# A two-layer block of attention, FP4 feed-forward and a recurrence: rounding's small steps in another form, zeros written by ScalarE, and another order of hand-written plans

## The chip, the cores and the metric

The kernel runs on one core of one Trainium2 chip. The core has five engines that run their own queues in order and wait for each other by semaphores: TensorE (PE, with its weight loads as PEld), VectorE (DVE), ScalarE (ACT), GpSimd (POOL) and SyncE (SP), which here only issues DMAs. The metric is the device time of one execution in microseconds; lower is better.

## What is computed

Sixteen sequences of 512 tokens with 256 channels, all in fp32, pass four steps, each with a residual and a LayerNorm behind it:

```
x = LN(x + attention(x))       16 heads, through 32 latents per head, rotary, causal softmax
x = LN(x + fp4_ffn(x))         256 -> 704 (gate, up) -> 256
x = LN(x + recurrence(x))      512 steps, one after the other, 16 heads x 64 states
x = LN(x + channel_mix(x))     three 256x256 products, token shift
```

The feed-forward rounds its inputs, its hidden values and its weights to FP4 in blocks of 16 values:

```python
scale = max(abs(block)) / 6, at least 1e-12
q = nearest of {0, .5, 1, 1.5, 2, 3, 4, 6} to abs(block / scale), with its sign, times scale
```

The recurrence is `state = tanh(state @ tanh(a) + x_t @ b)`; its result is `state @ c + skip * x_t`.

## The kernel before

**Two stages.** In the first, attention and feed-forward run over the sequences b = 0 to 15. In the second, the recurrence steps through time for all sequences at once and the channel mix runs beside it. Between them lies the rest of the last sequence's feed-forward. The result of the first stage goes through DRAM (`xs`) from one to the other.

**Slots.** A sequence's attention is 12 slots: four groups g of heads, each with three blocks n of query rows. A slot computes four heads' scores (`scores`, L524, into four PSUM banks), DVE adds the mask and finds the row's extreme (L536), ACT takes the exponentials (L549), TensorE turns the probabilities (`turn`, L559) one slot later, ACT copies them (L561), and behind a group's third block `weighted` multiplies with the values (L590). All products of this stage share seven PSUM banks, drawn by `mm`.

**Plans.** Between these steps, twice per head, `Beside.half_slot` puts in other work from a list written by hand: `PLAN_0` and `PLAN_1` for the first two sequences, `PLAN_15` for the last, `PLAN` for the thirteen between (b = 2 to 14). An entry is a kind of task, the sequence it belongs to as an offset, and a part: "U-1.2" is the next step of the feed-forward's first half (`ffn_up`) for tokens 256 to 383 of the sequence before this one. The kinds: L latents, H heads, V values, O output projection with LayerNorm (L497 to L504), Q quantization of the feed-forward's input, U gate and up products, D down product with LayerNorm (L331, L98) and the store to `xs` (L334), P a pause. A "U" has three entries: it transposes (ps_xq), then makes the first half's gate and up products (pg, pu), then the second half's. A "D" has two: transposes of the hidden values (ps_h, copied to hT), then the product (ps_d). An entry that has more than one step is called again at its next place in the list.

**What sets the order.** TensorE runs its instructions in the order in which the program is written (`manual_schedule`). The instructions of the other engines are ordered by a scheduler that takes what is ready by its own account, earlier lines first; so they may run well ahead of the place in the program at which they stand. `Q` only queues the rounding; its pieces are written out one per half slot by `vector_step`, and the rest at once by `vector_done` when a U or D step needs them.

**Rounding.** `fp4` (L181) is a chain on one engine after another: DVE takes the block maxima (L201), scales them and bounds them from below (L202), inverts (L203), multiplies by a constant just under 1 (L204), multiplies the data by the inverse (L207), makes a rounding constant (L209, L210) and adds it (L213); POOL subtracts it (L214) and multiplies by the scale (L215).

**LayerNorm.** DVE's statistics (L91, L92), POOL's reciprocal root (`rstd_of`, L84 and L86), and one DVE instruction for (x - mean) * rstd: L98 in `layernorm`, L502 in `out_projection`.

**Between the stages.** The list `FIRST` holds the steps for the last sequence that run before the recurrence: E quantize now, U and D as above, F wait for a hidden rounding, N the recurrence's first normalized tokens (`normed`). Then the recurrence's first input products (L1020) begin. `hist`, four tiles that hold states, is zeroed at L1008.

Of the kernel before, what the change touches and what calls it, by code (L numbers as in the profile page):

```python
# [10 lines left out]
F32 = mybir.dt.float32  # L11
# [3 lines left out]
AF = mybir.ActivationFunctionType  # L15
ALU = mybir.AluOpType
# [43 lines left out]
def tile_kernel(ctx: ExitStack, tc: tile.TileContext, I: dict, out: bass.AP):  # L60
# [8 lines left out]
    neg_half = const.tile([P, 4], F32, name="neg_half")  # L69
    nc.gpsimd.memset(neg_half, -0.5)  # L70
    cols = const.tile([P, NCOLS], F32, name="cols")
    nc.sync.dma_start(cols, I["cols"])
# [21 lines left out]
    def layernorm(dst, src):  # L94
        mv = small.tile([P, 4, 2], F32, tag="mv", name="mv")
        stats_into(mv[:, 0, :], src)
        rs = rstd_of(mv, 1, LN_EPS)
        nc.vector.tensor_scalar(dst, src, mv[:, 0, 0:1], rs[:, 0:1], ALU.subtract, ALU.mult)  # L98

# [81 lines left out]
    def fp4(dst, x, nb, rows=P):  # L181
# [13 lines left out]
        def blocks(t):  # L195
            return t.rearrange("p (n k) -> p n k", k=16)
# [4 lines left out]
        nc.vector.tensor_reduce(sc, blocks(x), AX.X, ALU.max, apply_absolute_value=True)  # L201
        nc.vector.tensor_scalar(sc, sc, 1.0 / 6.0, 1e-12, ALU.mult, ALU.max)  # L202
        nc.vector.reciprocal(inv, sc)  # L203
        nc.vector.tensor_scalar(inv, inv, 1.0 - 2.0**-23, None, ALU.mult)  # L204
        if n > C:
            yield
        nc.vector.tensor_tensor(blocks(q), blocks(x), over(inv), ALU.mult)  # L207
        yield
# [132 lines left out]
    with ExitStack() as a:  # L341
# [56 lines left out]
        vpad = [wts.tile([P, NT, H, 32], F32, name=f"vpad{i}") for i in range(2)]  # L398
        for i in range(2):
            nc.gpsimd.memset(vpad[i], 0.0)  # L400

# [80 lines left out]
        def out_projection(b):  # L482
# [3 lines left out]
            for j in range(0, NT, 2):  # L486
# [14 lines left out]
                for i in range(2):  # L501
                    nc.vector.tensor_scalar(  # L502
                        x[:, j + i, :], x[:, j + i, :], mv[:, i, 0:1], rs[:, i : i + 1],
                        ALU.subtract, ALU.mult,  # L504
                    )
# [110 lines left out]
        def pause(b):  # L616
# [15 lines left out]
        PLAN = [  # L632
            "L0.1", "L0.1", "U-2.3", "U-2.3", "H0", "H0", "O-1", "D-2.2", "L0.1", "O-1", "V1",
            "D-2.2", "L0.2", "L0.2", "L0.3", "Q-1.0", "L0.3", "Q-1.1", "L0.2", "U-1.0", "D-2.3",
            "U-1.1", "U-1.0", "U-1.0", "V1", "L0.3", "U-1.1", "Q-1.2", "H1", "U-1.2", "D-2.3",
            "Q-1.3", "U-1.2", "U-1.1", "U-1.2", "H1", "U-1.3", "D-1.0", "D-1.0", "D-1.1", "L1.0",
            "L1.0", "D-1.1", "L1.0",
# [14 lines left out]
        PLAN_15 = [  # L652
            "L0.1", "U-2.3", "U-2.3", "H0", "H0", "L0.1", "O-1", "D-2.2", "L0.1", "P0", "D-2.3",
            "L0.2", "D-2.2", "L0.3", "L0.2", "O-1", "Q-1.0", "U-1.0", "L0.2", "L0.3", "U-1.0", "P0",
            "P0", "Q-1.1", "U-1.0", "L0.3", "U-1.1", "U-1.1", "D-2.3", "Q-1.2", "Q-1.3", "P0",
            "U-1.2", "D-1.0", "U-1.3", "U-1.2", "P0", "U-1.1", "U-1.2", "D-1.0", "U-1.3", "U-1.3",
            "D-1.1", "D-1.1", "D-1.3", "D-1.2", "D-1.3", "D-1.2",
        ]
# [124 lines left out]
        ps_y = five.enter_context(tc.tile_pool(name="ps_y", bufs=1, space=PSUM))  # L783
        banks[:] = [ps_2] * 2 + [ps_b] * 5

        with tc.manual_schedule(engines={mybir.EngineType.PE}):
# [219 lines left out]
    for g in range(2):  # L1006
        for i in range(2):
            nc.gpsimd.memset(hist[g][i], 0.0)  # L1008
    state = [None, None]
# [65 lines left out]
    def beside(M):  # L1075
# [16 lines left out]
    FIRST = [  # L1092
        "E3", "U0", "U0", "E1", "U0", "U3", "U1", "U1", "D0", "E2", "F0", "D0", "U1", "U2", "N0",
        "U2", "U3", "F1", "U2", "N0", "F2", "U3",
    ]
# [203 lines left out]
```

## Time and profile before

| | |
|---|---|
| median of three runs | 2560.16 us (2558.01 to 2562.15) |
| the profiled execution | 2558.65 us, of it the span 2556.6 us |
| busy: PE, DVE, ACT, POOL | 2428.8, 1944.7, 1613.2, 1036.7 us |
| a middle sequence (892.9 to 1000.9) | 108.0 us, PE busy 105.99, DVE 89.00 |
| the last sequence (1650.6 to 1774.0) | 123.4 us, PE busy 112.63 |
| between the stages (1774 to 1828) | 54.0 us, PE busy 32.74 |
| the recurrence (1828 to 2556) | 728 us, PE busy 704.75, DVE 483.94 |

How to read it: times are microseconds from the span's start unless marked ns. A line of the order of time gives start, duration, engine, line, operation, out<-in, shapes and count; in brackets stand the engine's idle time before it and what ended that. A line of the groups gives, behind the count, busy microseconds and mean ns of one, then idle time before it and its releasers. A DVE or POOL instruction that waits for the other one's access to memory counts as busy while it waits. Matmuls are pipelined, and their ends are modelled. fp32 matmuls show as two instructions each.

### The profile page before, as it was taken

What the parts mean: (1) busy time and instruction counts of PE and PEld (TensorE: products, weight loads), DVE (VectorE), ACT (ScalarE), POOL (GpSimd) and SP (SyncE); (2) the same over time, 40 slices, a digit from 0 to 9 for tenths busy, and PEclk for the clock granted to TensorE, in tenths of its full rate; (3) what the DMA queues carried; (4) which work ended last, traced back from release to release, by engine and by line L of the source; (5) the groups of instructions that cost most, each with busy time, mean ns of one, the idle gap of its engine ahead of it and who ended that gap; (6) DMA issues with size and microseconds to landing.
All of it is one profiled execution on the core that took longest, in us unless ns stands there. A gap on an engine that the chain in (4) does not pass through costs nothing.

```text
span 2556.6 us, 73922 instructions
## 1 busy us (share of the span) xinstructions
PE 2428.8 (95%) x28802; PEld 1713.3 (67%) x28802; DVE 1944.7 (76%) x5621; ACT 1613.2 (63%) x5532; POOL 1036.7 (41%) x1649
## 2 busy tenths in 40 slices
PE   8789999999999999999999999997799999999998
PEld 4456666666666666666666666665578888888885
DVE  6767888788888888888787887877756666666666
ACT  4656666666666666667666666664266666666664
POOL 4322333333333333333333333333545555555554
PEclk9889999999999999999999999999899999999999
DMA  3000000000000000000000000000101111111100
GB/s 118 22 10 6 14 22 14 16 15 12 24 14 16 16 12 24 14 16 14 14 16 22 14 14 7 16 11 11 42 28 40 40 40 40 38 38 40 36 28 27
DMA packets 58016, 61.30 MB, mean 24 GB/s; under 512 B 7873, under 2 KB 53058, under 8 KB 57666
## 3 DMA queue, kind: packets, MB, share of 16 engines
q1 hardware_dynamic: 56802, 55.54, 7.1%
q8 instruction: 226, 3.70, 0.6%
q14 instruction: 124, 1.02, 0.1%
q10 hardware_dynamic: 864, 1.05, 0.1%
HBM read 39.79 MB, written 16.78 MB: 22 GB/s over the span
## 4 chain that ended last, share of the span: by engine, by line
PE 54%; DVE 28%; ACT 9%; POOL 5%; issue 3%; DMA 1%; ACTq 0%; DVEq 0%; POOLq 0%
PE u L1060 8%; DVE p L536 6%; PE ps_pt L559 5%; PE u L1020 5%; PE S L524 4%; ACT p L549 4%; PE py L590 3%; PE pg L160 3%; PE pu L160 3%; PE ps_h L439 3%; ACT pT L561 3%; DVE q_q L207 2%; PE ps_a L904 2%; PE ps_d L160 2%; DVE q_sc L201 2%
## 5 line engine op out<-in xcount | busy, mean ns | idle before, releaser
L549 ACT ACTIVATE p<-p,nm 128x512 f32<-128x512 f32 (+3 forms) x1024 | 569.9, 561 | 520.1 <-DVE nm L536 516.1
L1068 ACT ACTIVATE hist<-u 64x64 f32<-64x64 f32 x2048 | 445.5, 218 | 235.1 <-PE u L1060 153.0
L536 DVE CUSTOM_DVE_ANT_0 p<-S,mask 128x512 f32<-128x512 f32 (+3 forms) x1024 | 443.7, 483 | 50.2 <-PE S L524 50.2
L559 PEld LDWEIGHTS ps_pt<-ident,p 128*128 128x128 f32 x2560 | 296.5, 141 | 235.4 <-issue 85.5
L1060 PEld LDWEIGHTS u<-hist,ta 128*64 128x64 f32 x8176 | 367.3, 138 | 119.9 <-ACT hist L1068 40.7
L559 PE MATMUL ps_pt<-ident,p 128*128 128x128 f32 x2560 | 393.3, 280 | 9.0 <-DVE nm L536 3.5
L1060 PE MATMUL u<-hist,ta 128*64 128x32 f32 x8176 | 394.2, 218 | 4.6 <-ACT hist L1068 4.4
L561 ACT COPY pT<-ps_pt 128x384 f32<-128x384 f32 (+1 forms) x768 | 370.0, 515 | 39.2 <-PE ps_pt L559 38.9
L214 POOL TENSOR_TENSOR q_q<-q_q,q_m 128x256 f32<-128x256 f32 (+1 forms) x142 | 167.3, 1178 | 452.0 <-DVE q_q L213 434.4
L524 PE MATMUL S<-kc,qr 32*128 32x128 f32 (+3 forms) x2048 | 235.3, 474 | 8.9 <-ACT qr L478 7.9
L1020 PE MATMUL u<-xt,wb 128*64 128x64 f32 x4128 | 223.0, 230 | 2.4 <-issue 2.4
L549 ACT ACTIVATION_READ_ACCUMULATOR p<-p,nm 128x1 f32 x1024 | 199.3, 195 | 0.0
L160 PE MATMUL pg<-wgT,xqT 128*128 128x352 f32 x512 | 177.6, 470 | 4.1 <-ACT xqT L289 2.9
L473 POOL TENSOR_TENSOR qc<-qc,qs 128x512 f32<-128x512 f32 x64 | 81.5, 1274 | 236.3 <-DVE qs L472 231.3
L160 PE MATMUL pu<-wuT,xqT 128*128 128x352 f32 x512 | 172.8, 460 | 1.2 <-DVE th L304 1.2
L160 PE MATMUL ps_d<-wdT,hT 128*128 128x256 f32 x732 | 169.7, 381 | 2.2 <-ACT hT L323 2.2
L590 PEld LDWEIGHTS py<-pT,vpad 128*32 128x32 f32 x5120 | 141.2, 110 | 43.0 <-issue 30.7
L1020 PEld LDWEIGHTS u<-xt,wb 128*64 128x64 f32 x4128 | 164.9, 138 | 7.4 <-issue 3.0
L590 PE MATMUL py<-pT,vpad 128*32 128x128 f32 x5120 | 165.3, 276 | 3.8 <-ACT pT L561 3.5
L524 PEld LDWEIGHTS S<-kc,qr 32*128 32x128 f32 x2048 | 110.8, 185 | 78.0 <-issue 32.0
L84 POOL TENSOR_SCALAR ve<-mv 128x1 f32<-128x1 f32 (+1 forms) x160 | 32.6, 204 | 302.1 <-DVE mv L92 276.7
L160 PEld LDWEIGHTS ps_d<-wdT,hT 128*128 128x128 f32 x732 | 134.9, 191 | 19.6 <-ACT hT L323 3.1
(164 smaller groups left out, 4595.6 us busy)
## 6 DMA issues: line engine op xcount, KB each, us to landing
xT<-in_xT_dram SPq DMA_DIRECT2D x16, 512.0 KB
x<-in_x_dram SPq DMA_DIRECT2D x16, 512.0 KB
xs<-x SPq DMA_DIRECT2D x64, 128.0 KB
x<-xs SPq DMA_DIRECT2D x32, 256.0 KB
xm<-xs SPq DMA_DIRECT2D x32, 256.0 KB
out_dram<-o SPq DMA_DIRECT2D x64, 128.0 KB
w<-in_w_down_dram SPq DMA_DIRECT2D x2, 352.0 KB
w<-in_w_gate_dram SPq DMA_DIRECT2D x5, 128.0 KB
```

Of the source, the lines that this page charges most:

```text
L160: nc.tensor.matmul(dst, left, right, start=start, stop=stop)
L214: nc.gpsimd.tensor_tensor(q, q, m, ALU.subtract)
L473: nc.gpsimd.tensor_tensor(of[k], of[k], x, ALU.add)
L524: nc.tensor.matmul(S[h][:, at : at + w], q[rs, i * P : i * P + P], k[rs, :w], start=True, stop=True,)
L536: nc.vector.tensor_tensor_reduce(out=p[:, own], in0=S[h][:, own], in1=mask[:, T - (i + 1) * P :], scale=1.0, scalar=-MASKED, op0=ALU.add, ...
L549: nc.scalar.activation(p[:, own], p[:, own], AF.Exp, bias=nm[:, u : u + 1], scale=-1.0, accum_out=sum_of[b, g][:, cb, half, h : h + 1],)
L559: nc.tensor.transpose(ps[:, at : at + P], p[:, at : at + P], ident)
L561: nc.scalar.copy(pT[:, :w], ps[:, :w])
L590: nc.tensor.matmul(py[q * 32 : q * 32 + 32, PLACE[i][1], :], vpad[b % 2][:, j, g * 4 + h, :], pt, start=j == 0 and h % 2 == 0, stop=j == i ...
L1020: nc.tensor.matmul(u[rs, k, par:n:2, bs : bs + 16], wb[:, g * 2 + k, par, half, rs], xt[:, g, at : at + n - par : 2, :], start=par == 0 an ...
L1060: nc.tensor.matmul(into[cs, :, c, :], ta[:, t % 2, g * 2 + k, cs], own[:, :, c, :], start=False, stop=True, skip_group_check=True,)
L1068: nc.scalar.activation(state[g][rs, :, r * 32 : r * 32 + 32].rearrange("p k (s b) -> p k s b", s=2), u[rs, :, t - t0, :] .rearrange("p k ( ...
```

## The change

1. In `fp4`, L202 becomes a scalar_tensor_tensor with a constant tile `tiny` (1e-12) as its second tensor; L204 goes, and its constant moves into L207, which becomes a scalar_tensor_tensor. `tiny` is filled by one POOL memset at the start.
2. In `layernorm` and `out_projection`, L98 and L502 become scalar_tensor_tensor, with rstd spread over the row by a stride of zero as the second tensor.
3. The zeros of `vpad` (L400, POOL) are written further down in the program, just ahead of the loop over slots.
4. The zeros of `hist` (L1008) are written by ACT, as an Identity with scale 0 of the tile `ta`, instead of by POOL memsets.
5. `PLAN`, `PLAN_15` and `FIRST` get other orders. `PLAN` and `FIRST` hold the same entries as before; `PLAN_15` has one pause fewer.

```diff
+    tiny = const.tile([P, 44], F32, name="tiny")
+    nc.gpsimd.memset(tiny, 1e-12)
...
-        nc.vector.tensor_scalar(dst, src, mv[:, 0, 0:1], rs[:, 0:1], ALU.subtract, ALU.mult)
+        nc.vector.scalar_tensor_tensor(
+            dst, src, mv[:, 0, 0:1], rs[:, 0:1].to_broadcast([P, C]), ALU.subtract, ALU.mult
+        )
...
-        nc.vector.tensor_scalar(sc, sc, 1.0 / 6.0, 1e-12, ALU.mult, ALU.max)
+        nc.vector.scalar_tensor_tensor(sc, sc, 1.0 / 6.0, tiny[:rows, :nb], ALU.mult, ALU.max)
         nc.vector.reciprocal(inv, sc)
-        nc.vector.tensor_scalar(inv, inv, 1.0 - 2.0**-23, None, ALU.mult)
         if n > C:
             yield
-        nc.vector.tensor_tensor(blocks(q), blocks(x), over(inv), ALU.mult)
+        nc.vector.scalar_tensor_tensor(
+            blocks(q), blocks(x), 1.0 - 2.0**-23, over(inv), ALU.mult, ALU.mult
+        )
...
         vpad = [wts.tile([P, NT, H, 32], F32, name=f"vpad{i}") for i in range(2)]
-        for i in range(2):
-            nc.gpsimd.memset(vpad[i], 0.0)
...
-                    nc.vector.tensor_scalar(
-                        x[:, j + i, :], x[:, j + i, :], mv[:, i, 0:1], rs[:, i : i + 1],
-                        ALU.subtract, ALU.mult,
+                    nc.vector.scalar_tensor_tensor(
+                        x[:, j + i, :], x[:, j + i, :], mv[:, i, 0:1],
+                        rs[:, i : i + 1].to_broadcast([P, C]), ALU.subtract, ALU.mult,
                     )
...
         PLAN = [
-            "L0.1", "L0.1", "U-2.3", "U-2.3", "H0", "H0", "O-1", "D-2.2", "L0.1", "O-1", "V1",
-            "D-2.2", "L0.2", "L0.2", "L0.3", "Q-1.0", "L0.3", "Q-1.1", "L0.2", "U-1.0", "D-2.3",
-            "U-1.1", "U-1.0", "U-1.0", "V1", "L0.3", "U-1.1", "Q-1.2", "H1", "U-1.2", "D-2.3",
-            "Q-1.3", "U-1.2", "U-1.1", "U-1.2", "H1", "U-1.3", "D-1.0", "D-1.0", "D-1.1", "L1.0",
+            "L0.1", "L0.1", "U-2.3", "U-2.3", "H0", "H0", "O-1", "D-2.2", "L0.1", "D-2.2", "O-1",
+            "V1", "L0.2", "L0.2", "L0.3", "L0.3", "Q-1.1", "Q-1.0", "U-1.0", "L0.2", "U-1.1",
+            "D-2.3", "U-1.0", "U-1.0", "V1", "L0.3", "U-1.1", "H1", "Q-1.2", "U-1.2", "Q-1.3",
+            "D-2.3", "U-1.2", "U-1.1", "D-1.0", "U-1.2", "H1", "L1.0", "D-1.0", "D-1.1", "U-1.3",
             "L1.0", "D-1.1", "L1.0",
         ]
...
         PLAN_15 = [
-            "L0.1", "U-2.3", "U-2.3", "H0", "H0", "L0.1", "O-1", "D-2.2", "L0.1", "P0", "D-2.3",
-            "L0.2", "D-2.2", "L0.3", "L0.2", "O-1", "Q-1.0", "U-1.0", "L0.2", "L0.3", "U-1.0", "P0",
-            "P0", "Q-1.1", "U-1.0", "L0.3", "U-1.1", "U-1.1", "D-2.3", "Q-1.2", "Q-1.3", "P0",
-            "U-1.2", "D-1.0", "U-1.3", "U-1.2", "P0", "U-1.1", "U-1.2", "D-1.0", "U-1.3", "U-1.3",
-            "D-1.1", "D-1.1", "D-1.3", "D-1.2", "D-1.3", "D-1.2",
+            "L0.1", "L0.1", "U-2.3", "D-2.2", "U-2.3", "H0", "H0", "L0.1", "O-1", "D-2.2", "D-2.3",
+            "O-1", "L0.2", "Q-1.0", "U-1.0", "L0.3", "U-1.0", "Q-1.2", "Q-1.1", "L0.2", "L0.3",
+            "L0.2", "U-1.1", "P0", "P0", "U-1.0", "U-1.1", "U-1.2", "D-2.3", "U-1.2", "Q-1.3",
+            "L0.3", "U-1.3", "D-1.0", "U-1.1", "U-1.2", "D-1.0", "D-1.1", "U-1.3", "U-1.3", "D-1.1",
+            "P0", "D-1.2", "D-1.3", "D-1.2", "P0", "D-1.3",
         ]
...
         banks[:] = [ps_2] * 2 + [ps_b] * 5
+        for i in range(2):
+            nc.gpsimd.memset(vpad[i], 0.0)
...
     for g in range(2):
         for i in range(2):
-            nc.gpsimd.memset(hist[g][i], 0.0)
+
+            nc.scalar.activation(
+                hist[g][i].rearrange("p t k n -> p (t k n)"), ta.rearrange("p a k n -> p (a k n)"),
+                AF.Identity, scale=0.0,
+            )
...
     FIRST = [
-        "E3", "U0", "U0", "E1", "U0", "U3", "U1", "U1", "D0", "E2", "F0", "D0", "U1", "U2", "N0",
-        "U2", "U3", "F1", "U2", "N0", "F2", "U3",
+        "U0", "U0", "E1", "E3", "U0", "U3", "D0", "U1", "F0", "E2", "D0", "U1", "N0", "U2", "U1",
+        "F1", "U2", "U2", "U3", "U3", "F2", "N0",
     ]
```

## The prediction

> **What bounds the kernel now.** I read the page first (busy shares, then the chain that ended last), then busy time by stage, then who waits for whom in single stages, then the order of time where a stage's waits end.
>
> ```profile
> PE 2428.8 (95%) x28802; PEld 1713.3 (67%) x28802; DVE 1944.7 (76%) x5621; ACT 1613.2 (63%) x5532; POOL 1036.7 (41%) x1649
> ```
>
> TensorE is busy 95% of the span and nobody else over 76%. By stage (stretch, length, then busy time of PE, PE's weight loads, DVE, ACT and POOL, the granted clock, DMA):
>
> ```profile
> 892.90:1000.90 108.00, 105.99 (x850) 70.78 (x850) 89.00 (x266) 71.13 (x213) 37.40 (x45) 1.00 0.05 16
> 1650.60:1774.00 123.40, 112.63 (x961) 77.15 (x962) 93.44 (x283) 72.91 (x216) 38.98 (x49) 0.99 0.04 13
> 1774.00:1828.00 54.00, 32.74 (x110) 20.80 (x109) 40.45 (x98) 6.32 (x15) 22.81 (x30) 0.84 0.09 27
> ```
>
> A middle sequence (the first) takes 108 us and leaves TensorE 2.0 us idle; DVE has 19 us to spare. So TensorE bounds the thirteen sequences that PLAN orders, and VectorE's saving there is hidden unless TensorE waits for it. The last sequence leaves 10.8 us idle, the border between the stages (the rest of the last sequence's feed-forward) 21.3 of 54. From 1828 on is the recurrence, 728 us, which the change leaves alone. The gain can lie in three places only: 26 us of idle (plus part-idle, below) in the middle, 11 in the last sequence, 21 at the border.
>
> **The border.** In order of time:
>
> ```profile
> 1779.27 3.61 POOL L1008 MEMSET hist<- 128x1024 f32 x4
> 1779.36 3.98 DVE L502 TENSOR_SCALAR x<-x,mv,rstd 128x256 f32<-128x256 f32 x2 [0.43 <-POOL rstd L86]
> ...
> 1788.40 0.69 PE L287 MATMUL ps_xq<-ident,xq 128*128 128x128 f32 x2 [10.20 <-POOL xq L215]
> ```
>
> Two normalizations that take 0.41 us each elsewhere take 3.98 together: they sit until the four memsets end at 1782.88. TensorE waits 10.2 us for what follows. The chain that ended last runs through "POOL hist L1008 x4", 3.56 us. Moving the zeros to ACT removes the memsets: 3.98 becomes 2 x 0.475 = 0.95, so 3.0 us; one L204 less on this chain, 0.17. Gain 3.1. ACT pays 4 x 1.06 us (the 128x1024 ACTIVATE of ta took 1056 ns) but idles 14.7 us before its xqT copy at 1789; that covers the 4.2 us three times over. Without that cover it would cost up to 4.2, and the xqT copy would be late.
>
> FIRST's new order: U0's three steps, then D0 at once, before U1's products. In the trace D0's transposes waited 6.12 us for hq; ahead of them stood U1's products (2.63 us). Now only U3's transposes (0.4) stand there. hq comes after U0's last L307: 0.89+0.2+0.42+0.9+0.52+0.52+0.88 of DVE, 1.69+1.39 of POOL, some gaps: 7.8 us. It no longer shares DVE with U1's steps and x2's quantization (it took 9.6 us after the product's end, now 8.3). TensorE therefore waits about 8.0 instead of 6.1+0.5, but U1's 2.6 us are work that comes later and covers D0's normalization and its two transfers (L98's end at 1814.1 to the first L859 at 1819.1: 5.0 us). N0's transposes go last, so the L872 that fills xt (1.0 us) lies open before L1020. E3 goes behind E1: x3's rounding then fills DVE while U0's products run. Net -0.4, between -2.5 and +2. Moved with D0 is its store to xs on SP and the load after it; nothing else is queued on SP between them. **Border: -3.5 us.**
>
> **Rounding and normalizing on DVE.**
>
> ```profile
> L202 DVE TENSOR_SCALAR q_sc<-q_sc 128x44 f32<-128x44 f32 x66 | 27.7, 419 | 1.1
> L204 DVE TENSOR_SCALAR q_inv<-q_inv 128x16 f32<-128x16 f32 x74 | 31.2, 423 | 1.0
> L204 DVE TENSOR_SCALAR q_inv<-q_inv 128x44 f32<-128x44 f32 x66 | 24.0, 364 | 1.1
> L98 DVE TENSOR_SCALAR x<-x,mv,rstd 128x256 f32<-128x256 f32 x64 | 26.4, 413 | 74.1 <-POOL rstd L86 74.0
> L942 DVE SCALAR_TENSOR_TENSOR muk<-d,cols,x3T 128x256 f32<-128x256 f32 x64 | 28.0, 476 | 0.2
> ```
>
> L204's mean is 423 and 364 ns, its median 176: most of the mean is a wait for POOL inside the instruction. Two readings of that differ. If the new three-operand form never waits for POOL, the change saves L204 whole (55 us), L202's excess over 0.18 us (74 x 0.07 + 66 x 0.24 = 21 us) and L502's (mean 615, median 414: 64 x 0.2 = 13 us): 5.5 us per sequence. The Trainium skill, SBUF — State Buffer, section "Who interferes with whom", speaks against this: a DVE instruction with two SBUF inputs still contends with a GpSimd instruction that reads SBUF; only one that merely writes leaves it free. The trace agrees on an instruction with two SBUF inputs:
>
> ```profile
> 1804.41 1.38 POOL L215 TENSOR_TENSOR hq<-q_q,q_sc 128x704 f32<-128x704 f32 x1
> ...
> 1804.51 1.56 DVE L213 TENSOR_TENSOR q_q<-q_q,q_m 128x256 f32<-128x256 f32 x1
> ```
>
> This L213 takes 0.42 us when alone and 1.56 here, to just after POOL's end. All four new forms (L98, L202, L207, L502) read two SBUF tensors, and POOL's L214, L215 and L473 read SBUF. So I take it that the waits stay, or go on to L207 and L209, and that only L204's bare 0.16 to 0.18 us goes: 8 x 0.17 = 1.4 us per sequence.
>
> Against it stand the slower forms. By VectorE: DVE Perf Modes, section "The perf-mode tier table", fp32 tensor_scalar runs at twice the rate that a two-tensor operation has: 256/0.96/2 = 133 ns lost on each L98 and L502, 17 us in all. By the rows it is 476 - 413 = 63 ns, 8 us in all or 0.5 per sequence; I take the row. L207's constant is worth some 15 ns (L991 711 against L938 695). DVE nets -0.8 us per sequence, between -5.5 and +0.5, and nearly all of it lies under TensorE. Taken for the end: 0 in the middle, -1 us in sequences 0 and 1 together, where TensorE waits openly for quantized data (2.7 and 4.8 us for wq, 4.4 for xq).
>
> **vpad's zeros.** At the start L394's copy stood 5.9 us (3.43 to 9.30) while POOL ran memsets without a break, 3.54 us of them vpad's. If these go later, wqk's copies come up to 3.5 us sooner; but DVE's next work waits for w_gate's load until 13.84, and TensorE needs that DVE's turned_k at 16.97. No gain; if the memsets land beside the first quantizations, up to 3.5 us lost. wb's memset, of a much later sequence, already runs there at 7.22, so these probably stay near. Taken: 0; tiny's memset adds some 0.1 us to POOL (neg_half's took 0.10) before anything waits for it.
>
> **The middle order, 13 times.** Same steps, other places. Where TensorE is held in a middle sequence:
>
> ```profile
> 918.85 1.89 PE L421 MATMUL ps_v<-wv,xT 128*128 128x256 f32 x8
> 920.67 1.14 PE L524 MATMUL S<-kc,qr 32*128 32x512 f32 x8
> ...
> 922.13 2.76 PE L160 MATMUL ps_d<-wdT,hT 128*128 128x256 f32 x12
> 924.72 1.10 PE L559 MATMUL ps_pt<-ident,p 128*128 128x128 f32 x6
> 926.23 1.12 PE L457 MATMUL ps_q<-heads,bdq 64*128 64x512 f32 x2 [0.40 <-DVE nm L536]
> 927.04 1.12 PE L457 MATMUL ps_k<-heads,bdk 64*128 64x512 f32 x2
> ```
>
> ps_q waits 0.40 us because DVE got to the scores of 920.67 only at 924.54: O-1's second half sat before them. Having lost its pairing, q and k then take 1.93 instead of 1.12 us. PLAN now puts D-2.2's second step where O-1's second half stood, and O-1's after the scores: DVE is free for them some 2 us earlier, 1.2 us gained. Its price: hT's copies ended at 917.25, while TensorE would now come for them at 916.79: 0.5 us lost. Further on L1.0's first step goes ahead of D-1.0's second and D-1.1's first. Before, it waited 0.61 us (ACT pT) and left the next scores 1.80 us instead of 0.93; half of that 1.5 is taken, 0.7, since q and k now hold two PSUM banks while DVE is busy with h2. Q-1.2 now stands directly ahead of U-1.2, whose transposes came at 961.27, when xq was 1.07 us old: between 0 and 4 us (four half slots) of new wait; 0.4 is taken, as Q-1.0 directly ahead of U-1.0 in the last sequence's old plan met no wait. Sum per sequence: -1.2 + 0.5 - 0.7 + 0.4 = -1.0; **13 times: -13 us.** The DMAs issued by moved steps are L334's stores alone, on SP, with nobody waiting for them in this stage.
>
> **The last sequence.** D-2.2 now runs ahead of D-2.3 instead of overlapping it; that removes the 2.2 us for which ACT's hT copy waited on ps_d, and the 1.93 us for which a transpose waited on L331. On the other side L0.3 starts nine half slots, not five, ahead of L0.2's last product, and its q holds a bank until then (0.2 us of wait before, 1 to 2 possible). Of the tail's waits, 2.0 us on hT and 0.4 on DVE, one half should go: D-1.1's two steps now stand further apart. One pause fewer issues nothing. Sum: -1.9 (transpose), -0.4 (ACT's queue), -1.2 (tail), +1.0 (bank) = **-2.5 us**, between -7 and +3.
>
> **Sum.** -1 - 13 - 2.5 - 3.5 = -20. The profiled execution took 2558.65 us (span 2556.6, 2.05 around it): 2538.65; the median of the runs lies 1.5 higher, so **2540 us**.
>
> **Rivals.** (a) The new forms don't wait for POOL and the middle gives what TensorE loses: its 2.0 us idle and half of some 3.5 of broken pairings, 2.7 more per sequence: 2540 - 35 = 2505 to 2515. For it: DVE's "th" and "h" were late behind a stretched L204 (1.59) and L209 (1.37) when scores took 2.52 us at 958.33. Against it: L213 above. (b) The middle's gains and losses cancel: only border and last sequence, 2560 - 7 = 2553. For it: TensorE is 98% busy. (c) Slower: Q-1.2's place. If x2's rounding comes after its program place, U-1.2 waits 4 us, 13 x 3.6 = 47 more than taken: 2587. It makes the kernel slower by the 5 us below once the wait is 25/13 + 0.4 = 2.3 us per sequence. For it: xq was only 1.07 us early. Against it: the rounding of x0 and x1 ran 10 us ahead of its place. (d) The reform does nothing at all in DVE: same as the sum above, since little rests on it.
>
> **How the numbers follow.** 0.2% is 5 us, about what a measurement of this kernel can tell from no change. Likeliest, 0.50: 2540, its own range 2528 to 2553. (a) 0.14. (b) 0.18, of which 0.08 beyond 0.2% and 0.10 within. (c) and its like 0.18, from 2566 up. Faster 0.72, same 0.10, slower 0.18. The range takes in most of (a) and the milder part of (c): 2508 to 2570.
>
> **What would show it.** Right: no memset before L502 at the border and L502 near 0.48 us; the first ps_xq wait near 7 us instead of 10.2; a middle sequence near 107.0 us; L207 and L209 means above before's, with waits beside L214. Wrong: TensorE waiting for POOL's xq at U-1.2, or for hT at D-2.2, or L202 at its bare 0.18 us throughout.

## The result, and the profile after

The changed kernel takes 2541.53 us (median of four runs, 2540.61 to 2543.46), beside 2559.09 us for the kernel before on the same chip (four runs, 2557.99 to 2562.15): ratio 0.993, 95% interval 0.9913 to 0.9948, so 17.6 us less. 2540 was predicted. The sum was right and its parts were not. Lines below are those of the changed kernel, whose numbers differ by a few from before: L98 is now L100, L202 L206, L207 L210, L209 L214, L502 L505, L536 L539, L160 L164, L331 L336, L1020 L1029, and L204 is gone.

The busy shares on the page of after:

```profile
PE 2405.2 (95%) x28802; PEld 1710.4 (67%) x28802; DVE 1925.8 (76%) x5479; ACT 1621.0 (64%) x5536; POOL 1044.4 (41%) x1646
```

TensorE ran the same 28802 matmuls in 23.6 us less busy time. A busy time that shrinks at equal work was not work alone: two products that run one behind the other instead of side by side, for one, count longer (below).

Busy time by stage, after (stretch, length, then busy time of PE, its weight loads, DVE, ACT and POOL, the granted clock, DMA): one middle sequence, the last sequence with its attention's last products, the border up to the recurrence's first tanh, its first 32 steps, and sequence 0.

```profile
883.84:990.30 106.46, 103.60 (x848) 70.17 (x848) 88.61 (x258) 70.96 (x212) 37.78 (x44) 1.00 0.05 16
...
1629.09:1759.56 130.47, 119.67 (x976) 82.08 (x976) 95.46 (x281) 73.63 (x217) 39.61 (x49) 0.97 0.04 12
1759.56:1815.29 55.73, 31.85 (x134) 21.48 (x135) 37.51 (x92) 9.96 (x19) 25.07 (x31) 0.78 0.08 27
1815.29:1863.01 47.72, 43.88 (x938) 37.10 (x938) 29.14 (x73) 27.97 (x129) 28.29 (x58) 0.93 0.14 41
30.56:133.98 103.42, 88.23 (x647) 53.15 (x647) 70.50 (x224) 69.26 (x213) 33.73 (x39) 0.83 0.12 35
```

The same view of before, for sequence 0, the last sequence, the border and the first 32 steps, in the same cut:

```profile
30.99:129.71 98.72, 82.50 (x647) 51.07 (x647) 69.85 (x234) 68.66 (x213) 34.15 (x39) 0.90 0.12 37
...
1650.58:1778.20 127.62, 116.37 (x976) 79.77 (x976) 95.95 (x290) 73.30 (x217) 39.00 (x49) 0.99 0.04 13
1778.20:1829.62 51.42, 30.33 (x139) 19.54 (x141) 39.57 (x96) 5.95 (x14) 24.25 (x32) 0.83 0.09 29
1829.62:1881.40 51.78, 45.65 (x934) 37.47 (x932) 31.70 (x77) 27.85 (x128) 32.21 (x61) 0.90 0.13 38
```

Stage by stage, the two profiled executions differ like this:

| stage | before | after | change | predicted |
|---|---|---|---|---|
| start and sequence 0 | 129.7 | 134.0 | +4.3 | -1 (with sequence 1) |
| sequence 1 | 111.1 | 111.1 | 0 | |
| 13 middle sequences | 1409.8 (108.44 each) | 1384.0 (106.46) | -25.8 | -13 |
| last sequence | 127.6 | 130.5 | +2.9 | -2.5 |
| border | 51.4 | 55.7 | +4.3 | -3.5 with the next row |
| first 32 steps | 51.8 | 47.7 | -4.1 | |
| the rest | 675.2 | 675.8 | +0.6 | 0 |

The middle gave twice what was expected and paid for losses in three places where a gain was forecast. At the border the memsets are gone, as foreseen. After, in order of time (start, duration; in brackets idle time and what ended it), DVE, then POOL, then TensorE:

```profile
1760.72 0.88 DVE L505 SCALAR_TENSOR_TENSOR x<-x,mv,rstd 128x256 f32<-128x256 f32 x2 [0.43 <-POOL rstd L88]
...
1762.87 0.43 DVE L210 SCALAR_TENSOR_TENSOR q_q<-x,q_inv 128x256 f32<-128x256 f32 x1
1764.16 0.48 DVE L505 SCALAR_TENSOR_TENSOR x<-x,mv,rstd 128x256 f32<-128x256 f32 x1 [0.87 <-POOL rstd L88]
1764.56 0.28 DVE L214 TENSOR_SCALAR q_m<-q_q 128x256 uint32<-128x256 uint32 x1
...
1766.99 0.68 POOL L220 TENSOR_TENSOR xq<-q_q,q_sc 128x256 f32<-128x256 f32 x1
...
1767.72 0.69 PE L292 MATMUL ps_xq<-ident,xq 128*128 128x128 f32 x2 [8.16 <-POOL xq L220]
```

L505's pair takes 0.88 us instead of 3.98, so the 3.1 us were found. But of TensorE's wait only 10.20 - 8.16 = 2.0 went: L214 belongs to the rounding that TensorE waits for, and it now stands on DVE behind the next pair's L505, for whose rstd DVE idles 0.87 us. The stall moved one instruction down the queue.

VectorE's groups (count, then busy us, mean ns, idle before), after and then before:

```profile
L210 DVE SCALAR_TENSOR_TENSOR q_q<-x,q_inv 128x256 f32<-128x256 f32 x64 | 43.6, 684 | 1.0
L214 DVE TENSOR_SCALAR q_m<-q_q 128x256 uint32<-128x256 uint32 x74 | 43.1, 585 | 1.0
...
L206 DVE SCALAR_TENSOR_TENSOR q_sc<-q_sc,tiny 128x44 f32<-128x44 f32 x66 | 34.5, 523 | 1.5
L100 DVE SCALAR_TENSOR_TENSOR x<-x,mv,rstd 128x256 f32<-128x256 f32 x64 | 31.0, 485 | 55.3 <-POOL rstd L88 55.2
L505 DVE SCALAR_TENSOR_TENSOR x<-x,mv,rstd 128x256 f32<-128x256 f32 x64 | 28.4, 483 | 32.0 <-POOL rstd L88 32.0
```

```profile
L209 DVE TENSOR_SCALAR q_m<-q_q 128x256 uint32<-128x256 uint32 x74 | 35.5, 483 | 1.0
L207 DVE TENSOR_TENSOR q_q<-x,q_inv 128x256 f32<-128x256 f32 x64 | 27.4, 431 | 1.0
```

The waits for POOL did go on, from L204 to L207 (431 to 684 ns), L209 (483 to 585) and L202 (419 to 523).

### The profile page after: what moved, and what is told of

Same layout as the page of the kernel before. It is cut to its first block, busy times and chain, and to the rows that moved or that the text cites. A ratio compares the mean times of both kernels' runs of the same rounds, so it can differ in the third digit from the quotient of the medians.

```text
span 2538.8 us, 73782 instructions
## 1 busy us (share of the span) xinstructions
PE 2405.2 (95%) x28802; PEld 1710.4 (67%) x28802; DVE 1925.8 (76%) x5479; ACT 1621.0 (64%) x5536; POOL 1044.4 (41%) x1646
## 4 chain that ended last, share of the span: by engine, by line
PE 52%; DVE 28%; ACT 10%; POOL 5%; issue 4%; DMA 0%; DVEq 0%; POOLq 0%; ACTq 0%
PE u L1069 8%; DVE p L539 5%; PE ps_pt L562 5%; PE u L1029 5%; ACT p L552 4%; PE S L527 3%; PE ps_d L164 3%; DVE q_q L210 3%; PE pg L164 3%; PE pu L164 3%; PE ps_h L442 3%; ACT pT L564 3%; DVE q_q L218 2%; DVE q_sc L205 2%; PE ps_a L909 2%
## 5 line engine op out<-in xcount | busy, mean ns | idle before, releaser
L539 DVE CUSTOM_DVE_ANT_0 p<-S,mask 128x512 f32<-128x512 f32 (+3 forms) x1024 | 442.7, 483 | 52.6 <-PE S L527 52.1
L562 PEld LDWEIGHTS ps_pt<-ident,p 128*128 128x128 f32 x2560 | 301.7, 142 | 217.0 <-issue 105.9
L527 PE MATMUL S<-kc,qr 32*128 32x512 f32 (+3 forms) x2048 | 223.9, 475 | 10.5 <-ACT qr L481 7.9
L1029 PE MATMUL u<-xt,wb 128*64 128x64 f32 x4128 | 224.6, 231 | 5.8 <-issue 5.2
L164 PE MATMUL ps_d<-wdT,hT 128*128 128x256 f32 x732 | 172.8, 386 | 13.7 <-DVE nm L539 12.1
L164 PE MATMUL pg<-wgT,xqT 128*128 128x352 f32 x512 | 177.2, 469 | 7.7 <-DVE nm L539 5.1
L164 PE MATMUL pu<-wuT,xqT 128*128 128x352 f32 x512 | 174.6, 464 | 1.0 <-DVE nm L539 1.0
L1029 PEld LDWEIGHTS u<-xt,wb 128*64 128x64 f32 x4128 | 166.4, 140 | 10.6 <-issue 5.4
L164 PEld LDWEIGHTS ps_d<-wdT,hT 128*128 128x128 f32 x732 | 135.1, 191 | 37.1 <-DVE nm L539 15.4
L86 POOL TENSOR_SCALAR ve<-mv 128x2 f32<-128x2 f32 (+1 forms) x160 | 31.1, 195 | 311.7 <-DVE mv L94 309.0
L578 POOL COPY rcx<-rc 128x256 f32<-128x256 f32 x64 | 40.4, 631 | 287.3 <-DVE rc L576 259.5
```

Of the source, the lines that this page charges most:

```text
L164: nc.tensor.matmul(dst, left, right, start=start, stop=stop)
L527: nc.tensor.matmul(S[h][:, at : at + w], q[rs, i * P : i * P + P], k[rs, :w], start=True, stop=True,)
L539: nc.vector.tensor_tensor_reduce(out=p[:, own], in0=S[h][:, own], in1=mask[:, T - (i + 1) * P :], scale=1.0, scalar=-MASKED, op0=ALU.add, ...
L562: nc.tensor.transpose(ps[:, at : at + P], p[:, at : at + P], ident)
L1029: nc.tensor.matmul(u[rs, k, par:n:2, bs : bs + 16], wb[:, g * 2 + k, par, half, rs], xt[:, g, at : at + n - par : 2, :], start=par == 0 an ...
```

## The experiments

All times are medians, each with its ratio to the kernel before on the same chip; stages come from the profiled run of each kernel. Six kernels with the new PLAN and the new forms, alike in the middle, have middle sequences between 106.40 and 106.77 us, which says how finely this figure can be read. The other stages are coarser, each taken from one execution: sequence 0 takes 100.5 to 103.4 us in the changed kernel and runs 2, 3, 4, 6, 8 and 12, which are alike there, and the last sequence 129.1 to 132.9 in the changed kernel and runs 3, 8 and 12, which are alike in it.

| kernel | us | ratio (95%) | middle | last seq. | border | first 32 steps |
|---|---|---|---|---|---|---|
| before | 2559.1 | | 108.44 | 127.6 | 51.4 | 51.8 |
| changed | 2541.5 | 0.9930 (0.9913 to 0.9948) | 106.46 | 130.5 | 55.7 | 47.7 |
| 1 new PLAN alone | 2557.7 | 0.9994 (0.9986 to 1.0003) | 108.27 | 127.3 | 53.2 | 52.0 |
| 2 old PLAN_15 | 2542.9 | 0.9941 (0.9926 to 0.9956) | 106.54 | 130.6 | 54.9 | 47.4 |
| 3 old FIRST | 2545.6 | 0.9952 (0.9937 to 0.9967) | 106.74 | 129.1 | 49.6 | 58.5 |
| 4 both old | 2546.4 | 0.9952 (0.9937 to 0.9967) | 106.40 | 132.4 | 49.0 | 58.5 |
| 5 three new orders alone | 2566.1 | 1.0020 (1.0010 to 1.0029) | 108.14 | 129.8 | 59.1 | 49.0 |
| 6 three old orders | 2547.7 | 0.9948 (0.9933 to 0.9963) | 106.66 | 132.4 | 49.0 | 58.5 |
| 7 old forms in fp4 | 2571.8 | 1.0046 (1.0032 to 1.0060) | 108.83 | 132.1 | 56.2 | 49.0 |
| 8 hist by memset | 2543.9 | 0.9934 (0.9919 to 0.9949) | 106.77 | 129.8 | 55.2 | 49.4 |
| 9 L204 put back | 2572.6 | 1.0049 (1.0033 to 1.0064) | 108.83 | 133.9 | 57.2 | 48.0 |
| 10 only L204 gone | 2552.3 | 0.9971 (0.9959 to 0.9982) | 107.38 | 130.6 | 54.0 | 49.4 |
| 11 old normalizations | 2543.0 | 0.9929 (0.9917 to 0.9942) | 106.89 | 129.2 | 54.2 | 49.5 |
| 12 N0 earlier | 2548.1 | 0.9945 (0.9933 to 0.9958) | 106.68 | 132.9 | 53.0 | 56.8 |

### Which part of the change gave the middle's gain

**Run 1**, the kernel before with the new PLAN:

```diff
-            "L0.1", "L0.1", "U-2.3", "U-2.3", "H0", "H0", "O-1", "D-2.2", "L0.1", "O-1", "V1",
...
+            "L0.1", "L0.1", "U-2.3", "U-2.3", "H0", "H0", "O-1", "D-2.2", "L0.1", "D-2.2", "O-1",
...
```

> The kernel before with the new PLAN alone (order of the thirteen middle sequences). My theory: the middle gained 25.8 us (1.98 per sequence) because of the order itself, so this run takes about 2559 - 26 = 2533, between 2530 and 2537, and a middle sequence about 106.5 us; sequences 0 and 1 and the border stay as before (98.7, 111.1; first ps_xq of the border 10.2). Rival 1: the order gives only the 13 us that were predicted and the new rounding forms the other 13 (they shorten DVE's chain): about 2546, 107.4 per sequence. Rival 2: the new order pays only with the new forms: 2553 or more.

The theory that I had formed from the two traces fell at once: 0.17 us per sequence, no gain in the whole. By itself the order is worth next to nothing. It did take waits from TensorE, and made others. TensorE's waits over the thirteen sequences (total us, times, longest us), two of before, two of run 1 and one of the changed kernel:

```profile
PE ps_q L457 <- ACT pT L561: 8.0, 13, 0.6
PE ps_q L457 <- DVE nm L536: 5.2, 13, 0.4
...
PE ps_d L160 <- DVE nm L536: 17.6, 13, 1.4
PE ps_q L457 <- DVE nm L536: 2.3, 13, 0.2
...
PE ps_d L164 <- DVE nm L539: 12.1, 13, 1.0
```

What ps_q had waited for was nearly gone. In its place D-1.0's product, which now follows L1.0, waited up to 1.4 us in every sequence until DVE had read scores.

**Runs 5 and 6** complete the square: the three new orders in the old kernel (run 5), as the change has them, and the same edit backwards in the new one (run 6).

```diff
-            "L0.1", "L0.1", "U-2.3", "U-2.3", "H0", "H0", "O-1", "D-2.2", "L0.1", "O-1", "V1",
...
+            "L0.1", "L0.1", "U-2.3", "U-2.3", "H0", "H0", "O-1", "D-2.2", "L0.1", "D-2.2", "O-1",
...
-            "L0.1", "U-2.3", "U-2.3", "H0", "H0", "L0.1", "O-1", "D-2.2", "L0.1", "P0", "D-2.3",
...
+            "L0.1", "L0.1", "U-2.3", "D-2.2", "U-2.3", "H0", "H0", "L0.1", "O-1", "D-2.2", "D-2.3",
...
-        "E3", "U0", "U0", "E1", "U0", "U3", "U1", "U1", "D0", "E2", "F0", "D0", "U1", "U2", "N0",
...
+        "U0", "U0", "E1", "E3", "U0", "U3", "D0", "U1", "F0", "E2", "D0", "U1", "N0", "U2", "U1",
...
```

> The kernel before with the three new orders (PLAN, PLAN_15, FIRST) and nothing else: old forms on DVE, old zeros of hist and vpad. My theory after the first runs: the orders pay only together with the new forms. The middle stays at 108.3 us as with PLAN alone, the border keeps its memsets and its 10.2 us wait, so about 2555 to 2560, no different from before. Rival: the last sequence's and the border's new orders bring their part without the forms (the prediction's 2.5 and 0.4 us, or the 4.6 us by which the new FIRST was better beside the new forms): 2548 to 2552.

> The changed kernel with all three old orders: the new forms on DVE, ACT's zeros of hist and the moved zeros of vpad alone. Theory (form and order need each other): the middle stays near 108.2 us per sequence, the border gains 2 to 3 us, sequence 0 loses 2 to 5: about 2556 to 2560. Rival (the forms' 1.7 us per sequence is there under either order, since DVE is then earlier at the scores that TensorE waits for): the middle at 106.6 to 107.0 and the time at 2538 to 2545.

Forms and zeros alone (run 6) bring the middle to 106.66 and the time 0.52% below before: 13.3 us of the 17.9 that 0.70% makes. The rival was right in the middle; the time came out some 3 us above its band, since the first 32 steps took 58.5 us. So the new PLAN gives nothing that can be told apart beside the new forms either (106.66 lies within the spread). The orders together make the old kernel slower (1.0020). The new one stands at 0.9930 with them and 0.9948 without, and these intervals overlap: that the orders fit the new forms is likely, not shown.

**Run 7**, the old forms in the rounding alone:

```diff
-        nc.vector.scalar_tensor_tensor(sc, sc, 1.0 / 6.0, tiny[:rows, :nb], ALU.mult, ALU.max)
+        nc.vector.tensor_scalar(sc, sc, 1.0 / 6.0, 1e-12, ALU.mult, ALU.max)
         nc.vector.reciprocal(inv, sc)
+        nc.vector.tensor_scalar(inv, inv, 1.0 - 2.0**-23, None, ALU.mult)
...
-        nc.vector.scalar_tensor_tensor(
-            blocks(q), blocks(x), 1.0 - 2.0**-23, over(inv), ALU.mult, ALU.mult
-        )
+        nc.vector.tensor_tensor(blocks(q), blocks(x), over(inv), ALU.mult)
```

> The changed kernel with the old forms in fp4 alone (L202, L204, L207 as before; L98 and L502 keep the new form). Theory (L204's removal carries the middle's gain; in the trace of the new PLAN with the old forms, the two L204 and the L207 behind them put the scores' second head 0.2 to 0.4 us later at the place where TensorE waits for q and k): the middle goes back to 108.0 to 108.3 and the time to 2558 or so; sequence 0 comes back from 103.4 to about 98.7. Rival (L98 and L502, or DVE's order of instructions around them, carry it): the middle stays at 106.4 to 106.8 and the time at 2537 to 2541.

The rounding carries the gain: without it the middle is 108.83, half a microsecond beyond what the theory gave, and sequence 0 is back at 98.7 us. 108.83 is 0.56 more than run 1, which differs from it in the middle by the normalizations alone: their new form costs. L98's mean is 573 ns against 486 and L502's 482 against 410, four of each per sequence, 4 x 0.087 + 4 x 0.072 = 0.64 us of DVE, and TensorE loses nearly all of it.

**Runs 9 and 10** part the rounding: L204's own presence against the forms of L202 and L207. L204 is all that runs 7 and 10 differ in, and run 9 and the changed kernel. Run 9 is the changed kernel with

```diff
         nc.vector.reciprocal(inv, sc)
+        nc.vector.tensor_scalar(inv, inv, 1.0, None, ALU.mult)
```

> The changed kernel with a small instruction put back in L204's place (multiplies by 1.0; L202 and L207 keep the new forms). Theory (what the middle gains is L204's own stay on DVE, 0.4 to 0.5 us with its waits, ahead of scores that TensorE waits for): the middle goes back to 107.8 to 108.5 us per sequence, the time to 2559 or more. Rival (the gain is in the forms: an instruction with two SBUF inputs is held less by POOL than one with a single input): the middle stays at 106.5 to 107.0 and the time at 2542 to 2549.

and run 10 has the lines of run 7 but for the one at L204:

```diff
-        nc.vector.scalar_tensor_tensor(sc, sc, 1.0 / 6.0, tiny[:rows, :nb], ALU.mult, ALU.max)
+        nc.vector.tensor_scalar(sc, sc, 1.0 / 6.0, 1e-12, ALU.mult, ALU.max)
...
-        nc.vector.scalar_tensor_tensor(
-            blocks(q), blocks(x), 1.0 - 2.0**-23, over(inv), ALU.mult, ALU.mult
-        )
+        nc.vector.tensor_tensor(blocks(q), blocks(x), over(inv), ALU.mult)
```

> The changed kernel with the old L202 and L207 but without L204 (the constant factor just under 1 is left out of the rounding). Theory (L204's stay): the middle is at 106.3 to 106.7, as with the change, and the time at 2541, or 1 us less for the slightly cheaper L202 and L207. Rival (the forms): 108 per sequence and 2560.

One small instruction put back costs the whole gain and more: 108.83, as in run 7, so beside L204 the forms of L202 and L207 are worth nothing. Between runs 7 and 10 DVE's busy time differs by 1.56 us per sequence (89.61 and 88.05, overlaps counted once) and the sequence by 1.45. Run 10 still stands 0.9 above the change, between what the two theories said (its runs also spread widely, 2547 to 2559, the profiled one at 2548). The trace shows where. In run 9, DVE and TensorE at the fourth slot of the same sequence (b = 8), in order of time:

```profile
922.57 0.17 DVE L208 TENSOR_SCALAR q_inv<-q_inv 128x16 f32<-128x16 f32 x1
...
923.12 0.37 DVE L208 TENSOR_SCALAR q_inv<-q_inv 128x16 f32<-128x16 f32 x1
...
925.23 0.65 DVE L540 CUSTOM_DVE_ANT_0 p<-S,mask 128x512 f32<-128x512 f32 x1
...
926.96 0.83 DVE L100 SCALAR_TENSOR_TENSOR x<-x,mv,rstd 128x256 f32<-128x256 f32 x1 [1.07 <-POOL rstd L88]
927.71 0.68 DVE L540 CUSTOM_DVE_ANT_0 p<-S,mask 128x512 f32<-128x512 f32 x1
...
929.06 1.12 PE L461 MATMUL ps_q<-heads,bdq 64*128 64x512 f32 x2
929.67 1.12 PE L461 MATMUL ps_k<-heads,bdk 64*128 64x512 f32 x2
```

The same place in the changed kernel:

```profile
912.69 0.67 DVE L539 CUSTOM_DVE_ANT_0 p<-S,mask 128x512 f32<-128x512 f32 x1
...
914.01 0.68 DVE L539 CUSTOM_DVE_ANT_0 p<-S,mask 128x512 f32<-128x512 f32 x1
...
914.88 0.48 DVE L100 SCALAR_TENSOR_TENSOR x<-x,mv,rstd 128x256 f32<-128x256 f32 x1 [0.18 <-POOL rstd L88]
...
916.54 0.69 PE L460 MATMUL ps_q<-heads,bdq 64*128 64x512 f32 x1
916.63 0.69 PE L460 MATMUL ps_k<-heads,bdk 64*128 64x512 f32 x1
```

Counted from the same L505 (920.50 and 908.34), DVE reaches the first of these four scores 4.73 us later with L204 and 4.35 without: its two small instructions. Then, in run 9, the normalization L100 stands ahead of the second score and DVE idles 1.07 us for POOL's rstd; in the changed kernel it stands behind, and DVE idles 0.18. The second score comes 7.21 and 5.67 us after L505. TensorE's q and k then start 0.61 us apart instead of 0.09. Run 10 shows the same order as run 9, with its price:

```profile
916.26 0.83 DVE L100 SCALAR_TENSOR_TENSOR x<-x,mv,rstd 128x256 f32<-128x256 f32 x1 [1.07 <-POOL rstd L88]
917.01 0.68 DVE L537 CUSTOM_DVE_ANT_0 p<-S,mask 128x512 f32<-128x512 f32 x1
```

Over the middle, DVE idles 3.1 us per sequence ahead of this normalization in the changed kernel and 4.0 in runs 1, 7, 9, 10 and 11; the 0.9 is as much as run 10 lacks. So two things seem to add: L204's stay, about 1.45 us per sequence, which runs 7 and 10 show, and another place of one waiting instruction in DVE's queue, about 0.9, which is read from the traces, since no run moves that instruction alone. Why the scheduler puts it there with one form and not with another, no run here tells.

A plain sum stands behind this. The thirteen sequences in the view of the stages (length, then busy time of PE, its weight loads, DVE, ACT and POOL), of before, run 7, run 10, run 11, run 6 and the changed kernel:

```profile
240.82:1650.58 1409.76, 1378.71 (x11025) 921.13 (x11025) 1158.78 (x3466) 927.64 (x2774) 486.02 (x573) 1.00 0.05 15
...
246.33:1661.18 1414.85, 1371.66 (x11025) 916.14 (x11025) 1165.00 (x3466) 928.40 (x2774) 489.11 (x573) 1.00 0.05 15
...
240.47:1636.45 1395.98, 1357.33 (x11025) 914.81 (x11025) 1144.77 (x3362) 927.60 (x2774) 492.69 (x573) 1.00 0.05 16
...
242.99:1632.56 1389.57, 1350.60 (x11024) 910.95 (x11025) 1138.47 (x3362) 927.62 (x2774) 493.06 (x573) 1.00 0.05 16
...
245.03:1631.64 1386.61, 1368.28 (x11025) 923.29 (x11025) 1138.36 (x3362) 925.99 (x2774) 486.96 (x573) 1.00 0.05 16
...
245.12:1629.09 1383.97, 1345.28 (x11025) 912.26 (x11025) 1148.30 (x3362) 928.90 (x2774) 494.57 (x573) 1.00 0.05 16
```

Take DVE's busy time from the length, per sequence, and 19.1 to 19.4 us are left in eight of the fourteen kernels (before and runs 1, 5, 6, 7, 9, 10, 11), 18.1 to 18.4 in the six that have the new PLAN and all new forms. So the sequence is as long as DVE's busy time and a rest that keeps near one of two values; it does not follow TensorE's busy time, which is 105.25 us per sequence in run 6 and 103.48 in the changed kernel at nearly the same length. By the same sum run 10 has 1.2 us more rest than the changed kernel and 0.3 less DVE work, and run 6 and the changed kernel are alike by balance: 0.8 less work against 1.0 more rest.

**Run 11**, the old form of both normalizations:

```diff
-        nc.vector.scalar_tensor_tensor(
-            dst, src, mv[:, 0, 0:1], rs[:, 0:1].to_broadcast([P, C]), ALU.subtract, ALU.mult
-        )
+        nc.vector.tensor_scalar(dst, src, mv[:, 0, 0:1], rs[:, 0:1], ALU.subtract, ALU.mult)
```

(and L505 likewise)

> The changed kernel with the old forms of the normalizations L98 and L502 (one SBUF tensor, two pointers: 0.413 us against 0.482), the rest of the change kept, so no memset stands beside L502. Theory: 0.07 us on 8 instructions per sequence, less what POOL holds them again (L502's mean was 0.600 in the middle before, with waits): within 0.2 us per sequence of the change, 2539 to 2544. Rival (the new form of the normalizations matters as fp4's does, since only the old form waits for POOL): middle 107 or more, 2548 or more.

As fast as the change, as the theory said. DVE is 0.75 us per sequence less busy (87.57 against 88.32) but has the unlucky order (4.03 us of idle); the middle is 106.89, 0.43 above the change. The cheaper form and the better place have not been had together, so that remains untried.

### The last sequence and the border

**Runs 2, 3 and 4** put orders of before into the changed kernel. Run 2, PLAN_15:

```diff
-            "L0.1", "L0.1", "U-2.3", "D-2.2", "U-2.3", "H0", "H0", "L0.1", "O-1", "D-2.2", "D-2.3",
...
+            "L0.1", "U-2.3", "U-2.3", "H0", "H0", "L0.1", "O-1", "D-2.2", "L0.1", "P0", "D-2.3",
...
```

Run 3, FIRST, and run 4 both of these:

```diff
-        "U0", "U0", "E1", "E3", "U0", "U3", "D0", "U1", "F0", "E2", "D0", "U1", "N0", "U2", "U1",
-        "F1", "U2", "U2", "U3", "U3", "F2", "N0",
+        "E3", "U0", "U0", "E1", "U0", "U3", "U1", "U1", "D0", "E2", "F0", "D0", "U1", "U2", "N0",
+        "U2", "U3", "F1", "U2", "N0", "F2", "U3",
```

> The changed kernel with the last sequence's old order (PLAN_15 of before). My theory: the new order of the last sequence costs 2.9 us (130.5 against 127.6): this run takes about 2538.5, its last sequence 127 to 128 us, and TensorE's wait ahead of the border stays 8 to 10 us. Rival: the 2.9 us come from the new forms or from where the sequence before left off, not from PLAN_15: then the last sequence stays at 130 and the time at 2541.5, or grows to 2544 by the 2.5 us that the prediction credited to the new order.

> The changed kernel with the border's old order (FIRST of before). My theory: the 6.4 us more from the first ps_xq to the first state come from the new order, which leaves TensorE 9.5 us before D0's transposes and 5.2 us before the first input product; the first 32 steps give 4.1 us of it back. With the old order the stretch is 41 to 42 us, the first 32 steps 51 to 52, the sum 2 to 2.5 us shorter: 2539. Rival: the stretch is longer because of the new forms and of ACT's zeros: it stays above 45 us and the time at 2541.5 or, with the first steps losing their 4.1 us, 2545.

> The changed kernel with the old orders of the last sequence and of the border, so with the new PLAN, the new forms and ACT's zeros alone. My theory: the two losses are independent and add, 2541.5 - 2.9 - 2.3 = about 2536.5. Rival: they overlap (the border's start depends on where the last sequence ends its rounding), and this is no better than either alone, 2538.5 to 2540.

All three theories fell. Run 2's rival was right: PLAN_15 makes no difference of note beside the new forms: 130.6 and 130.5. The last sequence lost its 2.9 us with the old order too (run 6: 132.4). In the profile TensorE's busy time rose there from 116.4 to 119.7 us for the same 976 matmuls, at a clock of 0.97 instead of 0.99. The old FIRST does shorten the border by 6 us, as the theory said, and loses 11 in the next 32 steps: 4.6 us net for the new order in the profiles, 2545.6 against 2541.5 by the medians (ratios 0.9952 and 0.9930). Run 4 brought no sum of gains, there being none.

**Run 8**, memsets for hist beside the new form of L502:

```diff
-            nc.scalar.activation(
-                hist[g][i].rearrange("p t k n -> p (t k n)"), ta.rearrange("p a k n -> p (a k n)"),
-                AF.Identity, scale=0.0,
-            )
+            nc.gpsimd.memset(hist[g][i], 0.0)
```

> The changed kernel with hist zeroed by POOL's memsets again. The prediction's account (the normalization at L502 is held by the memsets): L502 at the border takes about 4 us for its pair again, the wait for the first ps_xq goes from 8.2 back to about 11, the time is 3 us longer, 2544.5. Rival (only the old form, with one SBUF tensor, is held by a memset; the new form reads two and, by the rule on who interferes with whom, is not held by an instruction that only writes): L502 stays near 0.5 us each, and the time at 2541.5.

The rival was right. Run 5, where the old form stood beside the same memsets (POOL's four ran from 1778.05 for 3.61 us):

```profile
1778.14 3.99 DVE L502 TENSOR_SCALAR x<-x,mv,rstd 128x256 f32<-128x256 f32 x2 [0.43 <-POOL rstd L86]
```

Run 8, POOL and then DVE:

```profile
1763.09 3.62 POOL L1013 MEMSET hist<- 128x1024 f32 x4
...
1763.18 0.88 DVE L505 SCALAR_TENSOR_TENSOR x<-x,mv,rstd 128x256 f32<-128x256 f32 x2 [0.44 <-POOL rstd L88]
...
1765.99 0.86 DVE L214 TENSOR_SCALAR q_m<-q_q 128x256 uint32<-128x256 uint32 x1
```

The new form runs its bare 0.48 us each in the middle of the memsets, while L214, a tensor_scalar with one SBUF tensor, is held until they end at 1766.71. One input is not what holds it: L205's reduction and L93's statistics, with one SBUF tensor too, ran in 0.41 and 0.42 us beside the same memsets. This is the rule of the Trainium skill, SBUF — State Buffer, "Who interferes with whom": an instruction with two SBUF inputs contends with a GpSimd instruction that reads, not with one that only writes, and tensor_scalar is among those that can contend. The change removed one stall twice over: either the form or ACT's zeros does most of it. With the new form beside memsets (run 8) the first ps_xq waits 9.0 us; with the old form beside ACT's zeros (run 11) L502's pair takes 0.73 us and the wait is 7.9; with both it is 8.2, with neither 10.2 (11.1 in run 5). The whole times of run 8 and the change can't be told apart.

**Run 12**, the one attempt at something better. TensorE waited 5.24 us before the first input product, with N0 last in FIRST:

```diff
-        "F1", "U2", "U2", "U3", "U3", "F2", "N0",
+        "F1", "U2", "U2", "U3", "N0", "U3", "F2",
```

> The changed kernel with the second N0 of FIRST one place ahead of the last U3 instead of last. In the changed kernel the three fills of xt (L872) stood behind a rounding and two normalizations on DVE, from 25.16 to 27.01 us of the border's stretch, while their transposes were done at 22.0, and TensorE waited 5.24 us before the first input product. Theory: that wait falls by the 2.5 us that U3's products take, and the stretch from the first ps_xq to the first state becomes 45 us instead of 47.6; since the hidden roundings that then fill the recurrence's first steps come no earlier, a half of it is given back there: about 2540. Rival: all is given back in the first 32 steps (47.7 becomes 50): 2541.5.

The wait fell to 2.92 and the border to 53.0, and the first 32 steps went from 47.7 to 56.8, worse than the rival. The later N0 steps now wait for POOL in the recurrence's start (TensorE in order of time):

```profile
1821.14 0.89 PE L888 MATMUL ps_xn<-ident,xn 128*128 128x128 f32 x4 [1.64 <-POOL xn L872]
...
1828.20 1.15 PE L888 MATMUL ps_xn<-ident,xn 128*128 128x128 f32 x4 [3.76 <-POOL xn L872]
```

and around these waits the clock goes. Busy time of PE, granted clock, DMA, in stretches of 6 us of run 12:

```profile
1822.50:1828.50 6.00, 2.24 (x40) 0.50 0.16 44
1828.50:1834.50 6.00, 6.00 (x66) 0.50 0.33 88
1834.50:1840.50 6.00, 6.00 (x132) 0.87 0.02 5
```

1.64 and 3.76 us are 5.4. In the second row TensorE is busy for all 6.00 us at half the clock and gets through 66 matmuls, against 132 in the third at 0.87 (their sizes differ; eight of L1029 took 0.67 us at 1829.73, and 0.43 at full clock in the changed kernel). So the wait is charged again. Run 3, with the old FIRST, shows the same: two waits of 3.98 and 3.28 us for POOL's xn, and a clock of 0.50 for 12 us. The Trainium skill, TensorE: Matmul & The Clock Gate, "What's actually happening", says that activity releases the throttle and that idleness brings back half rate; these rows agree.

## Why the prediction was right, and where only its sum was

**Right in the sum by luck: two errors cancel.** Predicted -20 from the profiled execution, measured -18.0 (2558.65 to 2540.61). The middle gave 12.8 us more than forecast, and the rest lost 8.0 us where 7 were to be gained.

- **Rounding in the middle, taken as 0: wrong**, and the largest error. "Nearly all of it lies under TensorE" was read from TensorE's 98%. The size of DVE's saving was well judged (1.4 us per sequence for L204; 1.56 by runs 7 and 10), and so was where POOL's waits would go. But L204 stands in DVE's queue ahead of scores whose banks TensorE needs, and it passes through almost one to one: 1.45. DVE's 19 us of slack per sequence was not there to be used: it stayed at 18 to 19 us, whatever DVE saved. The forms are worth -1.8 us per sequence under either PLAN, some -23 us.
- **The middle order, -13: wrong.** It measured -0.17 per sequence alone and nothing to be told beside the forms. The step that failed is "1.2 us gained" at ps_q: with the new PLAN alone, its wait fell from 0.40 to 0.19 us but q and k stayed one behind the other (run 1: 0.81 us apart). The pairing came back only when DVE's queue had lost L204 and the order of L98 had turned; and run 6, without it, is as fast in the middle. The 0.7 taken for L1.0's earlier step failed too: its 0.61 us of wait for pT went, and D-1.0's product waited 1.35 us in its stead (run 1). Of the terms against the order, hT's 0.5 us was 0.1, and Q-1.2's wait at U-1.2 did not come.
- **The forms' price.** The row (63 ns) was nearer than the estimate drawn from the Trainium skill, VectorE: DVE Perf Modes, "The perf-mode tier table" (133 ns): 72 ns on L502 and L98 alike. But it was put under TensorE as well, and it costs 0.56 us per sequence (runs 7 and 1).
- **Sequences 0 and 1, -1: wrong in sign.** Sequence 0 takes 98.6 to 98.7 us in the five kernels that have an L204, and 100.5 to 103.4 in all nine without; its granted clock went from 0.90 to 0.83 in the change. The sum had no term for the clock. What makes the clock drop there is not settled.
- **The last sequence, -2.5: wrong.** The waits named did go from their places: the 1.93 us on L331, and the tail's. Others of their size came (1.60 at ps_o, 1.60 at S, 1.22 at ps_ks, and 1.45 at ps_h, again for L331's sum, now L336): TensorE idles 11.3 us before and 10.8 after. With the new forms the old order is no faster (run 2).
- **The border, -3.5.** hist's 3.1 us was right as a cost, and mis-sized as a gain (2.0), because L214 fell behind the next rstd. That the form alone would free L502 from the memsets followed from the rule that the prediction itself cites, and was not drawn. FIRST's -0.4 was -4.6 net beside the new forms (in the profiles), the order's two waits (9.50 us for hq, 5.24 before the input products) as foreseen but larger, and a faster start of the recurrence not foreseen.
- **vpad's zeros, 0; ACT's zeros hidden: nothing speaks against them.** The start took 30.6 against 31.0 us; no run moved vpad's zeros alone.
- **Rivals.** (c) fell. (a) was near in its mechanism's effect (the middle gains more than its order), though not for its reason. Of what was to show the prediction right, L502 at 0.48 us and the means of L207 and L209 came true; the middle sequence was 106.46, below 107.0, and the first ps_xq wait 8.2, above 7.

## What to carry to other kernels

An engine's busy share does not say that another engine's savings are hidden: look at what stands in that other engine's queue just ahead of the results that the busy one needs, for there a saved microsecond passes through one to one even at 98%. When several edits come together, don't credit the one whose mechanism is easiest to tell: run each alone, since here the order looked like the cause in two traces and gave nothing alone. And in a stretch where TensorE has waits of several microseconds, price the clock after the wait, not the wait alone.

## What the runs showed of the hardware

- A scalar_tensor_tensor with two SBUF inputs ran in its bare 0.48 us beside POOL's memsets; a tensor_scalar with one took 3.67 us beside them (run 5) and 0.41 where ACT wrote the zeros (run 11).
- Two 64-row matmuls that start 0.09 us apart in the changed kernel ran one behind the other, 0.61 us apart, where TensorE had idled as little as 0.06 us before the first (run 10), and the lost overlap counts as TensorE's busy time. The same 11025 matmuls of the thirteen sequences were busy for 1378.7 us before, 1345.3 in the changed kernel, and 1368.3 in run 6, whose sequences are as short as the changed kernel's.
- Around two waits close together the granted clock stood at 0.50 for 12 us (3.98 and 3.28 us in run 3, 1.64 and 3.76 in run 12). A single wait of 5.24 us in the changed kernel left it at 0.74 over the next 6 us and full after that; what decides between the two was not tried.
